# Image-ahead first convolution, one ring for streamed filters and softmax sums by way of HBM in a convolution and attention block

## Chip, core and metric

The kernel runs on one core of a Trainium2 chip. The metric is the device time of one execution in microseconds (us); the times of several runs are compared by their median. Engines are named as the profile names them: PE (matmul), DVE (vector), ACT (activation), POOL and SP (which here issue transfers, POOL also small operations).

## What is computed

Eight images of 512 channels and 32 x 32 pixels, all in float32. Each is group-normalised, sent through a block of convolutions with two attention bottlenecks, and added to its input:

```python
t = cbs(x, cv1_w, cv1_bn, 0)            # 1x1, 512 -> 512; cbs = conv, batch norm, silu
ys = [t[:, :C], t[:, C:]]               # C = 256
for i in range(N):                      # N = 2
    yi = ys[-1]
    z = cbs(yi, m_cv1_w[i], m_cv1_bn[i], 1)          # 3x3, 256 -> 256
    z = bot_attention(z, m_qkv_w[i], m_rw[i], m_rh[i])   # 4 heads of 64, 1024 pixels
    z = jax.nn.silu(bn_eval(conv2d(z, m_cv2_w[i], 0), m_cv2_bn[i]))
    ys.append(yi + z)
y = cbs(jnp.concatenate(ys, axis=1), cv2_w, cv2_bn, 0)   # 1x1, 1024 -> 512
# outside: x = x + y, with y computed from the group-normalised x
```

## The kernel before

Channels lie on the 128 partitions, pixels along the free dimension, in halves of 512 columns. The eight images are unrolled; the order on each engine is made by a scheduler from the code, and the engines run their queues in order. A matmul in float32 is two passes on PE.

Per image the stages are: `gn_stats`, `gn_mean`, `gn_apply` (group norm; L300 to L325: statistics on DVE, two small matmuls gm_ps and gv_ps on PE with `gmat`, a power on POOL, then xn on DVE); `cv1` (L519: 32 matmuls of 512 columns, then silu); two times `bottleneck` (L529); `cv2` (L585: 64 matmuls), which adds x and stores. cv1 makes y0, and y1 in a padded tile `ypad[0]`.

In a bottleneck, `rows_in` (L234) transforms the padded rows on DVE into `v_in`, one tile for each of two input chunks of 128 channels, and the 3x3 convolution is 72 matmuls of 256 columns per output chunk pair (L545) with transformed filters `u`, which are made once (L175 to L193), kept in HBM and streamed through a ring of four slots. `project` (L332) makes q, kr and vT. `attention_fast` (L369) has four groups, one for each head pair and half of the queries, of eight key blocks, taken in pairs: `logits` (PE l_ps, ACT exp into `pt`, DVE adds into `acc`), `times_v` (PE av_ps, then ACT and DVE move it to `ao`), and `divide` (L424 on), which sums `acc` over the keys by matmuls with `ones` (s_ps, L432), adds the halves, keeps their largest and smallest value (smax, smin), takes the reciprocal and multiplies `ao`. Then `m2_ps` (L570) is the 1x1 convolution behind the attention, silu and the addition of the bottleneck's input.

`pt`, `v_in` and xn share a ring of three slots (tag pt). PSUM holds three tiles of two banks (tag big) and one (tag av, for av_ps, c3_end and the group norm). At the end smax and smin decide whether a general path, with the row maximum taken off, is run; with these inputs it is not.

SP issues the loads of x and u, ACT those of the other weights at the start, POOL the stores. The next image's x is loaded and its statistics taken between the output chunks of cv2 (`between`).

Of the kernel before, what the change touches and what calls it, by code (L numbers as in the profile page):

```python
# [49 lines left out]
def kernel(  # L51
# [123 lines left out]
    for n in range(N):  # L175
        for k in range(NM):
            raw = const.tile([P, 9, C], F32, tag="u", name="raw", bufs=4)
            nc.sync.dma_start(raw, m_cv1_w[n, ts(k, P)])
            for oc in range(NM):
                g0, g1, g2 = (raw[:, 3 * r : 3 * r + 3, ts(oc, P)] for r in range(3))  # L180
                u = const.tile([P, NPOS, 3, P], F32, tag="u", name="u_new", bufs=4)
                tmp = act.tile([P, 3, 3, P], F32, tag="pt", name="u_tmp", bufs=3)
                even, odd, wide = tmp[:, 0], tmp[:, 1], tmp[:, 2]
                nc.scalar.mul(u[:, 0], g0, 6.0)
                nc.scalar.mul(u[:, 5], g2, 24.0)
                nc.scalar.mul(odd, g1, -4.0)
                nc.vector.tensor_tensor(even, g0, g2, ALU.add)
                nc.vector.scalar_tensor_tensor(u[:, 1], even, -4.0, odd, ALU.mult, ALU.add)
# [538 lines left out]
```

## Time and profile before

| | |
|---|---|
| Median of 3 runs | 2894.04 us (2889.86 to 2895.5) |
| The profiled execution | 2889.72 us |
| Its span, first to last instruction | 2888.1 us |
| Granted PE clock, mean | 0.971 of full |
| PE busy | 2621.9 us (91%) |
| DVE busy | 1671.8 us (58%) |
| ACT busy | 949.0 us (33%) |
| POOL busy | 73.8 us (3%) |
| Moved by DMA | 130.81 MB |

The span is one profiled execution; its own time is 1.6 us above the span and 4.3 below the median of the runs. Busy times are sums over the span. Ends of matmuls are modelled, so rows of PE overlap by a few tenths; starts and waits are what is read. In a row of the timeline the first number is the start, the second the length, and what stands in brackets is the idle time of that engine before it and what ended it. The number behind a line's mean in the groups is the duration of one instruction in nanoseconds.

### The profile page before, as it was taken

What the parts mean: (1) busy time and instruction counts of PE and PEld (TensorE: products, weight loads), DVE (VectorE), ACT (ScalarE), POOL (GpSimd) and SP (SyncE); (2) the same over time, 40 slices, a digit from 0 to 9 for tenths busy, and PEclk for the clock granted to TensorE, in tenths of its full rate; (3) what the DMA queues carried; (4) which work ended last, traced back from release to release, by engine and by line L of the source; (5) the groups of instructions that cost most, each with busy time, mean ns of one, the idle gap of its engine ahead of it and who ended that gap; (6) DMA issues with size and microseconds to landing.
All of it is one profiled execution on the core that took longest, in us unless ns stands there. A gap on an engine that the chain in (4) does not pass through costs nothing.

```text
span 2888.1 us, 32855 instructions
## 1 busy us (share of the span) xinstructions
PE 2621.9 (91%) x13858; PEld 1319.9 (46%) x13858; DVE 1671.8 (58%) x2244; ACT 949.0 (33%) x1273; POOL 73.8 (3%) x180
## 2 busy tenths in 40 slices
PE   2988999899998999989999899998999989999897
PEld 1636346263463534545355443545345353463633
DVE  5384834847348564575546665466744757438482
ACT  1242422424223332333324242242522515224242
POOL 2000000000000000000000000000000000000000
PEclk9999999999999999999999999999999999999999
DMA  9201011010110101101011000101012010110000
GB/s 357 82 1 66 1 58 66 1 66 1 59 66 1 67 15 44 66 13 54 29 37 59 33 34 30 62 34 62 5 44 79 3 66 1 51 66 1 1 1 31
DMA packets 25084, 130.81 MB, mean 45 GB/s; under 512 B 4449, under 2 KB 4961, under 8 KB 15201
## 3 DMA queue, kind: packets, MB, share of 16 engines
q1 hardware_dynamic: 14400, 97.00, 9.4%
q0 software_dynamic: 6784, 26.25, 2.4%
q10 hardware_dynamic: 3744, 5.37, 0.5%
q8 instruction: 111, 1.82, 0.3%
q14 instruction: 45, 0.36, 0.0%
HBM read 102.40 MB, written 26.21 MB: 45 GB/s over the span
## 4 chain that ended last, share of the span: by engine, by line
issue 57%; PE 26%; DVE 13%; POOL 1%; DMA 1%; ACT 1%; DVEq 0%; POOLq 0%; ACTq 0%; SPq 0%
PE ps L229 12%; PE c_mid L545 6%; DVE acc L401 5%; PE c_end L545 3%; DVE rs L445 3%; PE l_ps L391 2%; PE av_ps L414 2%; PE v_ps L360 2%; DVE acc L398 1%; POOL out_dram L606 1%; DVE rs L441 1%; DVE smin L444 1%; DVE ao L447 1%; ACT pt L395 1%; DVE s L438 1%
## 5 line engine op out<-in xcount | busy, mean ns | idle before, releaser
L395 ACT ACTIVATE pt<-l_ps 128x1024 f32<-128x1024 f32 x512 | 483.0, 1031 | 159.0 <-PE l_ps L391 157.1
L401 DVE TENSOR_TENSOR acc<-acc,pt 128x1024 f32<-128x1024 f32 x384 | 470.2, 1224 | 68.0 <-ACT pt L395 33.7
L414 PE MATMUL av_ps<-pt,vT 64*64 64x512 f32 x4096 | 472.7, 591 | 25.8 <-DVE ao L422 25.8
L391 PE MATMUL l_ps<-q,kr 64*64 64x512 f32 x4096 | 463.3, 590 | 0.0
L545 PE MATMUL c_mid<-v_in,u 128*128 128x256 f32 x1536 | 353.2, 387 | 81.3 <-DVE v_in L265 66.8
L545 PEld LDWEIGHTS c_mid<-v_in,u 128*128 128x128 f32 x1536 | 295.2, 193 | 137.5 <-issue 95.4
L414 PEld LDWEIGHTS av_ps<-pt,vT 64*64 64x64 f32 x4096 | 153.4, 133 | 319.2 <-issue 260.8
L391 PEld LDWEIGHTS l_ps<-q,kr 64*64 64x64 f32 x4096 | 154.5, 132 | 286.7 <-issue 204.3
L229 PE MATMUL ps<-xn,cv_sb 128*128 128x512 f32 x512 | 233.4, 617 | 50.4 <-DVE xn L325 50.4
L214 ACT ACTIVATE h<-ps,bh,sh 128x512 f32<-128x512 f32 x128 | 92.5, 772 | 514.4 <-PE ps L229 514.4
L229 PE MATMUL ps<-z,qkv_sb 128*128 128x512 f32 x512 | 229.2, 595 | 0.2 <-DVE z L558 0.2
L229 PE MATMUL ps<-ypad,cv_sb 128*128 128x512 f32 x512 | 224.9, 592 | 0.0
L445 DVE RECIPROCAL rs<-rs 128x512 f32<-128x512 f32 x64 | 214.6, 3353 | 2.2
L229 PEld LDWEIGHTS ps<-xn,cv_sb 128*128 128x128 f32 x512 | 99.1, 196 | 178.7 <-issue 116.5
L545 PE MATMUL c_end<-v_in,u 128*128 128x256 f32 x768 | 176.1, 382 | 0.0
L545 PEld LDWEIGHTS c_end<-v_in,u 128*128 128x128 f32 x768 | 148.1, 193 | 22.1
L229 PEld LDWEIGHTS ps<-ypad,cv_sb 128*128 128x128 f32 x512 | 97.3, 190 | 122.5 <-issue 122.5
L279 DVE TENSOR_TENSOR sd<-c_mid,m 128x512 f32<-128x512 f32 x32 | 22.1, 692 | 223.3 <-ACT m L277 223.3
L229 PEld LDWEIGHTS ps<-z,qkv_sb 128*128 128x128 f32 x512 | 95.9, 190 | 106.8 <-issue 95.7
L570 PE MATMUL m_ps<-ao,m_sb 128*128 128x512 f32 x256 | 143.7, 714 | 0.9 <-DVE ao L447 0.9
L600 DVE SCALAR_TENSOR_TENSOR t<-t,h 128x512 f32<-128x512 f32 x64 | 41.4, 688 | 164.3 <-ACT t L215 164.3
L351 DVE TENSOR_TENSOR kr<-ps,rw_sb 128x512 f32<-128x512 f32 x64 | 41.2, 686 | 160.4 <-PE ps L229 160.4
(104 smaller groups left out, 2123.7 us busy)
## 6 DMA issues: line engine op xcount, KB each, us to landing
u<-u SPq DMA_DIRECT2D x64, 1152.0 KB, 6.9
x<-in_x_dram SPq DMA_DIRECT2D x32, 512.0 KB, 4.2
out_dram<-t POOLq DMA_DIRECT2D x64, 256.0 KB, 4.3
u<-u_new POOLq DMA_DIRECT2D x8, 1152.0 KB, 7.6
raw<-in_m_cv_w_dram SPq DMA_DIRECT2D x4, 1152.0 KB, 7.8
cv_sb<-in_cv_w_dram ACTq DMA_DIRECT2D x1, 2048.0 KB, 13.5
qkv_sb<-in_m_qkv_w_dram ACTq DMA_DIRECT2D x2, 768.0 KB, 13.1
cv_sb<-in_cv_w_dram ACTq DMA_DIRECT2D x1, 1024.0 KB, 9.4
```

What stands on the lines that cost most here:

```text
L214: nc.scalar.activation(h, ps, AF.Identity, scale=sh[:, k : k + 1], bias=bh[:, k : k + 1])
L229: nc.tensor.matmul(ps[:, half, :], w_of(k), rhs_of(k, half), start=(k == 0), stop=(k == nk - 1))
L351: nc.vector.tensor_tensor(dst, img(ps[:, half, :]), rw, ALU.add)
L360: nc.tensor.matmul(ps[:, j, :], z[:, k, ts(j0 + j, P)], qkv_sb[:, n, k, 2 * C : 3 * C], start=(k == 0), stop=(k == NM - 1),)
L391: nc.tensor.matmul(ps[kh * HD : (kh + 1) * HD, hd, :], kr[r, c, o : o + HD], q[r, c, ts(half, HALF)], start=True, stop=True,)
L395: nc.scalar.activation(pt[:, i], ps, AF.Exp, scale=SCALE)
L401: nc.vector.tensor_tensor(accs[g], accs[g], pt[:, i], ALU.add)
L414: nc.tensor.matmul(avs[g][hd * HD : (hd + 1) * HD, kh, :], vT[r, j, o : o + HD], pt[r, i, hd, :], start=(j == 0), stop=(j == NJ - 1),)
L445: nc.vector.reciprocal(rs, rs)
L545: nc.tensor.matmul(dst, us[k][:, pos, dx, :], vs[k][:, pos, :, dx : dx + F], start=(i == 0), stop=(i == NM * 3 - 1),)
L570: nc.tensor.matmul(pss[oc][:, half, :], m2_sb[:, n, k, ts(oc, P)], ao[:, k, ts(half, HALF)], start=(k == 0), stop=(k == NM - 1),)
L600: nc.vector.scalar_tensor_tensor(t, t, 1.0, h, ALU.add, ALU.mult)
```

## The change

The kernel is rewritten around four things. The normalisation writes into x's own tiles, and `cv1` takes a list of output chunks. Group norm, the load of cv1's filters, and the y1 half of the next image's cv1 are placed in the present image's first attention (`behind`: a table from group number to a function that is called there), the y0 half behind its `m2`; `rows_in` for the next image stands ahead of cv2. There is a third padded tile, since y1 of two images is alive.

cv1's and cv2's filters no longer stay in SBUF: they, `u` and the new `u_new` share one ring of four slots, and are loaded for each image. Filter transforms are made when first needed, from raw pieces in the pt ring. cv2 reads x again for the residual, through POOL's queue.

In `divide`, for all groups but the last of an attention, one row per head of the sums goes to HBM, comes back with 8 sums on each of 128 partitions, is added and inverted there, goes to HBM again and returns broadcast over the 64 partitions of a head. The last group keeps the reciprocal on 128 x 512 and sends its sums only for the final range check. Pairs are taken one ahead (logits of pair i, then the product of pair i - 1) in place of two and two.

```diff
-    xs = [load_x(act, 0, c, 5) for c in range(NX)]
+    xs = [load_x(act, 0, c, NX) for c in range(NX)]
+    def ring(shape, name):
+        return const.tile(shape, F32, tag="u", name=name, bufs=4)
+    def load_w1(q):
+        w = ring([P, NX, 2 * C], "w1")
+        q.dma_start(w, cv1_w.rearrange("(k p) o -> p k o", p=P))
+        return w
+    def load_w2():
+        nk = (2 + N) * NM // 2
+        ws = [ring([P, nk, C2], f"w2_{i}") for i in range(2)]
...
+    def make_u(n, oc, k):
+        raw = act.tile([P, 9, P], F32, tag="pt", name="raw", bufs=3)
+        nc.sync.dma_start(raw, m_cv1_w[n, ts(k, P), :, ts(oc, P)])
...
         def gn_mean(mv):
-            ps = ps_av.tile([P, NX], F32, tag="av", name="gm_ps")
+            ps = ps_big.tile([P, NX], F32, tag="big", name="gm_ps")
...
-            xn = []
-            for half in range(NH):
-                t = act.tile([P, NX, HALF], F32, tag="pt", name="xn", bufs=n_pt)
...
+            for c in range(NX):
+                nc.vector.tensor_scalar(
+                    xts[c], xts[c], gm[:, c : c + 1], gr[:, c : c + 1], ALU.subtract, ALU.mult
+                )
...
-                ps = act.tile([P, HALF], F32, tag="rs", name="s_0", bufs=2)
-                nc.scalar.copy(ps, sums[:, 0])
-                nc.vector.tensor_tensor(ps, sums[:, 1], ps, ALU.add)
                 rs = act.tile([P, HALF], F32, tag="rs", name="rs", bufs=2)
+                dst = ao[:, c, ts(half, HALF)]
                 i = at + g
-                nc.vector.tensor_scalar(
-                    rs, ps, 1.0, None, ALU.mult, ALU.max, accum_out=smax[:, i : i + 1]
-                )
-                nc.vector.tensor_reduce(smin[:, i : i + 1], rs, AX.X, ALU.min)
-                nc.vector.reciprocal(rs, rs)
-                dst = ao[:, c, ts(half, HALF)]
+                s_dram = tc.dram_tile([2, 2, HALF], F32, name=f"s_dram{i}")
+                rows = [act.tile([P, HALF], F32, tag=t, name="s_row", bufs=2) for t in ("h", "t")]
+                for kh, row in enumerate(rows):
+                    nc.scalar.copy(row, ps[:, kh, :])
+                    for hd in range(2):
+                        nc.sync.dma_start(s_dram[kh, hd : hd + 1, :], row[hd * HD : hd * HD + 1, :])
+                if last:
+                    nc.vector.tensor_tensor(rs, ps[:, 1, :], rows[0], ALU.add)
+                    nc.vector.reciprocal(rs, rs)
+                cs = small.tile([P, 2, QP], F32, tag="cs", name="cs", bufs=2)
+                nc.sync.dma_start(cs, s_dram.rearrange("k h (i r) -> (h i) k r", r=QP))
+                nc.vector.tensor_tensor(sums_all[:, i, :], cs[:, 0], cs[:, 1], ALU.add)
+                if not last:
+                    rc = small.tile([P, QP], F32, tag="rc", name="rc", bufs=2)
+                    nc.vector.reciprocal(rc, sums_all[:, i, :])
+                    r_dram = tc.dram_tile([2, HALF], F32, name=f"r_dram{i}")
+                    nc.sync.dma_start(r_dram.rearrange("h (i r) -> (h i) r", r=QP), rc)
+                    for hd in range(2):
+                        nc.sync.dma_start(
+                            rs[hd * HD : (hd + 1) * HD, :], r_dram[hd : hd + 1, :].to_broadcast([HD, HALF])
+                        )
                 nc.vector.tensor_tensor(dst, dst, rs, ALU.mult)
-            RUN = 2
-            for i in range(0, len(pairs), RUN):
...
+            for i in range(len(pairs) + 1):
+                if i < len(pairs):
+                    logits(pairs[i])
+                if i > 0:
+                    times_v(pairs[i - 1])
+                    g, j0 = pairs[i - 1][0]
+                    if j0 == 0:
+                        if g > 0:
+                            divide(g - 1)
+                        behind.get(g, lambda: None)()
+            behind.get(len(groups), lambda: None)()
             divide(len(groups) - 1)
...
+            def residual(oc, half):
+                t = act.tile([P, HALF], F32, tag="xr", name="x_res", bufs=2)
+                nc.gpsimd.dma_start(t, rows_of(x, oc, half))
...
+    s.group_norm(xs)
+    us = {(0, 0): make_u(0, 0, 0), (0, 1): make_u(0, 0, 1), (1, 0): make_u(0, 1, 0)}
+    y0 = new_y0()
+    s.cv1(w1, xs, y0, ypad[0], [*Y1S, *Y0S])
+    vs = [s.rows_in(ypad[0], k) for k in range(NM)]
+    load_bottleneck(0)
     for b in range(B):
...
+        z = s.conv3x3(0, vs, u_of(0))
...
+        if more:
+            xs = [load_x(act, b + 1, c, NX) for c in range(NX)]
+        def ahead():
+            nonlocal w1
+            if more:
+                s.group_norm(xs)
+                w1 = load_w1(nc.sync)
+            for oc, k in ((0, 0), (0, 1), (1, 0)):
+                us[oc, k] = get_u(1, oc, k)
+        def first():
+            nonlocal nxt
+            if more:
+                nxt = new_y0()
+                s.cv1(w1, xs, nxt, y1n, Y1S)
+        ao = s.attention_fast(0, z, b * N * NM * NH, {1: ahead, NM * NH: first})
+        s.m2(0, ao, y1, lambda oc, half: inner(y2, oc, half))
         if more:
+            s.cv1(w1, xs, nxt, y1n, Y0S)
+        vs = [s.rows_in(y2, k) for k in range(NM)]
+        z = s.conv3x3(1, vs, u_of(1))
...
+        ao = s.attention_fast(1, z, (b * N + 1) * NM * NH, {1: ahead})
+        ylast = act.tile([P, NM, HW], F32, tag="v", name="ylast")
+        s.m2(1, ao, y2, lambda oc, half: ylast[:, oc, ts(half, HALF)])
+        if more:
+            vs = [s.rows_in(y1n, k) for k in range(NM)]
+        s.cv2(b, w2, y0, y1, y2, ylast)
```

How the order of the engines' queues moves is shown at three places; line numbers are those of each kernel. First, DVE in the middle of an attention of the kernel before, where one group is divided among the next group's additions:

```order
L398 TENSOR_TENSOR acc<-pt 128x1024
L401 TENSOR_TENSOR acc<-acc,pt 128x1024 x2
L438 TENSOR_TENSOR s_2319<-s_ps,s_2319 128x512
L441 TENSOR_SCALAR rs,smax<-s_2319 128x512
L444 TENSOR_REDUCE smin<-rs 128x1
L445 RECIPROCAL rs<-rs 128x512
L447 TENSOR_TENSOR ao<-ao,rs 128x512
L401 TENSOR_TENSOR acc<-acc,pt 128x1024 x4
```

And DVE of the change at the same place, in a second attention (cs: the sums come back from HBM, rc: their reciprocals, rs: those broadcast):

```order
L429 TENSOR_TENSOR acc<-acc,pt 128x1024 x4
L479 TENSOR_TENSOR sums_all<-cs 128x8
L482 RECIPROCAL rc<-sums_all 128x8
L429 TENSOR_TENSOR acc<-acc,pt 128x1024 x2
L489 TENSOR_TENSOR ao<-ao,rs 128x512
L426 TENSOR_TENSOR acc<-pt 128x1024
L450 TENSOR_TENSOR ao<-av_ps,ao 128x512
```

The division is now in two short pieces, each behind a transfer, and the multiply (L489) stands ahead of the next group's first addition (L426) and of the addition that empties av_ps (L450).

Second, PE at the end of a first attention, of the kernel before (l_ps logits, av_ps product with v, s_ps sums, m_ps the 1x1 convolution behind, c_mid and c_end the 3x3 convolution):

```order
L391 MATMUL l_ps<-q,kr 64x512 x16
L414 MATMUL av_ps<-pt,vT 64x512 x16
L432 MATMUL s_ps<-acc,ones 64x512 x4
L570 MATMUL m_ps<-ao,m_sb 128x512 x8
L545 MATMUL c_mid<-v_in,u 128x256 x3
```

And of the change (ps is the next image's cv1, w its filters):

```order
L419 MATMUL l_ps<-q,kr 64x512 x8
L442 MATMUL av_ps<-pt,vT 64x512 x16
L255 MATMUL ps<-x,w_2473 128x512 x16
L461 MATMUL s_ps<-acc,ones 64x512 x4
L606 MATMUL m_ps<-ao,m_sb 128x512 x6
L255 MATMUL ps<-x,w_2473 128x512 x2
L606 MATMUL m_ps<-ao,m_sb 128x512 x2
L255 MATMUL ps<-x,w_2473 128x512 x14
L584 MATMUL c_mid<-v_in,u 128x256 x24
```

Sixteen matmuls of the next image now stand between the last product and the last sum, and sixteen more around and behind m_ps, ahead of the 3x3 convolution.

Third, DVE of the change at the end of a second attention, from the last pair's additions on (w_tmp and v_in are the next image's rows):

```order
L429 TENSOR_TENSOR acc<-acc,pt 128x1024
L280 SCALAR_TENSOR_TENSOR w_tmp<-ypad_110 128x512
L489 TENSOR_TENSOR ao<-ao,rs 128x512
L283 TENSOR_TENSOR w_tmp<-ypad_110 128x512
L284 TENSOR_TENSOR w_tmp<-ypad_110 128x512
L291 TENSOR_TENSOR v_in<-w_tmp 128x8x32
L292 TENSOR_TENSOR v_in<-w_tmp 128x8x32
L293 SCALAR_TENSOR_TENSOR v_in<-w_tmp 128x8x32
L294 SCALAR_TENSOR_TENSOR v_in<-w_tmp 128x8x32
```

Two more of v_in follow, then the addition that empties av_ps and the last division; in the kernel before these rows stood behind cv1, at the 3x3 convolution.

## Rows read from the trace of the kernel before

**Rows 1.** Page, part 1: busy time, share of the span, instructions of each engine.
```profile
PE 2621.9 (91%) x13858; PEld 1319.9 (46%) x13858; DVE 1671.8 (58%) x2244; ACT 949.0 (33%) x1273; POOL 73.8 (3%) x180
```

**Rows 2.** Timeline of PE, second image: start, length, instruction, idle before it.
```profile
440.65 1.46 PE L545 MATMUL c_mid<-v_in,u 128*128 128x256 f32 x6
...
446.51 9.30 PE L545 MATMUL c_mid<-v_in,u 128*128 128x256 f32 x42 [1.81 <-issue]
...
527.40 1.95 PE L414 MATMUL av_ps<-pt,vT 64*64 64x512 f32 x16 [0.70 <-DVE ao L422]
...
543.09 1.95 PE L414 MATMUL av_ps<-pt,vT 64*64 64x512 f32 x16 [0.86 <-DVE ao L422]
...
547.43 3.61 PE L391 MATMUL l_ps<-q,kr 64*64 64x512 f32 x32
550.86 3.61 PE L414 MATMUL av_ps<-pt,vT 64*64 64x512 f32 x32
558.26 1.09 PE L432 MATMUL s_ps<-acc,ones 64*64 64x512 f32 x8 [3.78 <-DVE acc L401]
...
576.64 2.90 PE L545 MATMUL c_mid<-v_in,u 128*128 128x256 f32 x6 [8.33 <-DVE v_in L265]
...
756.18 3.60 PE L229 MATMUL ps<-ylast,cv_sb 128*128 128x512 f32 x8
759.61 0.28 PE L306 MATMUL gm_ps<-mv,gmat 128*128 128x4 f32 x2
760.74 0.39 PE L317 MATMUL gv_ps<-dev,gmat 128*128 128x4 f32 x2 [0.85 <-DVE dev L312]
763.17 29.57 PE L229 MATMUL ps<-xn,cv_sb 128*128 128x512 f32 x64 [2.05 <-DVE xn L325]
792.58 1.46 PE L545 MATMUL c_mid<-v_in,u 128*128 128x256 f32 x6
```

**Rows 3.** Timeline of PE's weight loads: the sixth m2 matmul of the first attention.
```profile
566.33 0.30 PEld L570 LDWEIGHTS m_ps<-ao,m_sb 128*128 128x128 f32 x2 [0.77 <-DVE ao L447]
```

**Rows 4.** Stretches behind two waits: busy times, then PEclk, DMA share, GB/s.
```profile
558.30:568.40 10.10, 10.01 (x24) 3.63 (x24) 6.53 (x7) 1.46 (x3) 0.00 (x0) 0.83 0.00 0
...
576.70:580.60 3.90, 3.90 (x11) 3.16 (x12) 3.87 (x11) 0.00 (x0) 0.00 (x0) 0.56 0.00 0
```

**Rows 5.** Groups by line and shape: count, busy us, mean ns, idle before.
```profile
L445 DVE RECIPROCAL rs<-rs 128x512 f32<-128x512 f32 x64 | 214.6, 3353 | 2.2
...
L215 ACT ACTIVATE t<-h 128x512 f32<-128x512 f32 x192 | 113.4, 625 | 2.0
...
L214 ACT ACTIVATE h<-ps,bh,sh 128x512 f32<-128x512 f32 x128 | 92.5, 772 | 514.4 <-PE ps L229 514.4
...
L398 DVE TENSOR_TENSOR acc<-pt 128x1024 f32<-128x1024 f32 x64 | 78.1, 1220 | 87.8 <-ACT pt L395 87.8
...
L447 DVE TENSOR_TENSOR ao<-ao,rs 128x512 f32<-128x512 f32 x64 | 44.3, 692 | 2.2
...
L437 ACT COPY s<-s_ps 128x512 f32<-128x512 f32 x64 | 37.5, 585 | 174.9 <-PE s_ps L432 174.9
...
L325 DVE TENSOR_SCALAR xn<-x,gm,gr 128x512 f32<-128x512 f32 x64 | 31.5, 553 | 8.1 <-POOL gr L320 8.1
...
L188 DVE SCALAR_TENSOR_TENSOR u_new<-u_tmp 128x384 f32<-128x384 f32 x8 | 4.4, 555 | 3.0 <-DMA u<-u_new 2.9
```

**Rows 6.** Timeline of the start: the bn power on POOL, cv1's first matmuls on PE.
```profile
19.02 3.10 POOL L162 TENSOR_TENSOR rstd<-rstd,mhalf 128x16 f32<-128x16 f32 x1 [4.53 <-DVE rstd L161]
...
56.99 3.78 PE L229 MATMUL ps<-xn,cv_sb 128*128 128x512 f32 x4 [33.14 <-DVE xn L325]
```

**Rows 7.** Page, part 6: issues of x, KB each, median us to landing.
```profile
x<-in_x_dram SPq DMA_DIRECT2D x32, 512.0 KB, 4.2
```

**Rows 8.** Transfers of u issued in 590:594, one load of 1152 KB.
```profile
DMA to landing us min/median/max: 5.0/5.0/5.0
```

**Rows 9.** Transfers of out in 2825:2889, eight stores of 256 KB.
```profile
DMA to landing us min/median/max: 2.3/3.1/3.7
```

More of the change, by code (lines that the diff above doesn't have):

```diff
@@ L149 @@
     ypad = []
-    for n in range(N):
+    for n in range(N + 1):
         yp = const.tile([P, NM, F + 2, F], F32, name=f"ypad{n}")
@@ L174 @@
     ]
[L175 to L188, printed above, removed]
-                nc.vector.scalar_tensor_tensor(u[:, 2], even, -4.0, odd, ALU.mult, ALU.subtract)
-                nc.vector.scalar_tensor_tensor(wide, g2, 4.0, g0, ALU.mult, ALU.add)
-                nc.vector.scalar_tensor_tensor(u[:, 3], g1, 2.0, wide, ALU.mult, ALU.add)
-                nc.vector.scalar_tensor_tensor(u[:, 4], g1, -2.0, wide, ALU.mult, ALU.add)
-                nc.gpsimd.dma_start(u_dram[n][oc][k], u)
@@ new lines, in make_u @@
+    def make_u(n, oc, k):
+        raw = act.tile([P, 9, P], F32, tag="pt", name="raw", bufs=3)
+        nc.sync.dma_start(raw, m_cv1_w[n, ts(k, P), :, ts(oc, P)])
+        g0, g1, g2 = (raw[:, 3 * r : 3 * r + 3, :] for r in range(3))
+        u = ring([P, NPOS, 3, P], "u_new")
+        tmp = act.tile([P, 3, 3, P], F32, tag="wt", name="u_tmp", bufs=1)
+        even, odd, wide = tmp[:, 0], tmp[:, 1], tmp[:, 2]
+        nc.scalar.mul(u[:, 0], g0, 6.0)
+        nc.scalar.mul(u[:, 5], g2, 24.0)
+        nc.scalar.mul(odd, g1, -4.0)
+        nc.vector.tensor_tensor(even, g0, g2, ALU.add)
+        nc.vector.scalar_tensor_tensor(u[:, 1], even, -4.0, odd, ALU.mult, ALU.add)
+        nc.vector.scalar_tensor_tensor(u[:, 2], even, -4.0, odd, ALU.mult, ALU.subtract)
+        nc.vector.scalar_tensor_tensor(wide, g2, 4.0, g0, ALU.mult, ALU.add)
+        nc.vector.scalar_tensor_tensor(u[:, 3], g1, 2.0, wide, ALU.mult, ALU.add)
+        nc.vector.scalar_tensor_tensor(u[:, 4], g1, -2.0, wide, ALU.mult, ALU.add)
+        nc.gpsimd.dma_start(u_dram[n][oc][k], u)
+        return u
@@ L425, in divide @@
                 c, half = groups[g]
-                sums = ps_big.tile([P, 2, HALF], F32, tag="big", name="s_ps")
+                last = g + 1 == len(groups)
+                ps = ps_big.tile([P, 2, HALF], F32, tag="big", name="s_ps")
                 acc = accs.pop(g)
@@ L577, in bottleneck @@
                     nc.vector.scalar_tensor_tensor(t, t, 1.0, h, ALU.add, ALU.mult)
-                    if n == N - 1:
-                        dst = ylast[:, oc, ts(half, HALF)]
-                    else:
-                        dst = inner(ypad[n + 1], oc, half)
-                    nc.vector.tensor_tensor(dst, t, inner(yi, oc, half), ALU.add)
-            return ylast
-        def cv2(b, y0, ylast, xts, between):
+                    nc.vector.tensor_tensor(dst_of(oc, half), t, inner(yi, oc, half), ALU.add)
@@ L620 @@
+    vs = [s.rows_in(ypad[0], k) for k in range(NM)]
+    load_bottleneck(0)
+    nxt = None
     for b in range(B):
-        y0 = s.cv1(xn)
-        for n in range(N):
-            at = (b * N + n) * NM * NH
-            ylast = s.bottleneck(n, lambda n, z: s.attention_fast(n, z, at))
         more = b + 1 < B
-        if more:
-            nxt = [load_x(act, b + 1, 0, 5)]
-            mv = small.tile([P, NX, 2], F32, tag="mv", name="mv", bufs=2)
-        def between(oc):
-            if not more:
-                return
-            if oc > 0:
-                s.gn_stats(mv, oc - 1, nxt[oc - 1])
-            if oc + 1 < NX:
-                nxt.append(load_x(act, b + 1, oc + 1, 5))
@@ L648 @@
+    nc.vector.tensor_reduce(ends[:, 1:2], flat_sums, AX.X, ALU.min)
     good = const.tile([P, 1], F32, name="good")
```

168 lines of the change are left out of this document (88 added, 80 removed).

## Prediction

> **What bounds the kernel now.** I read the page first, then the PE timeline of the second image, then the clock in its stretches, then the costliest groups by line, and last the start and the DMA landings. The page [rows 1] shows PE busy for 91% and DVE for 58%; a share over stages of unlike limits does not say where PE waits, so the timeline decides. One image lasts from its first 3x3 convolution at 440.65 to the next one's at 792.58, 351.9 us [rows 2]. The reader is to see there that PE waits at five places: 1.81 inside the first 3x3 convolution, 0.70 and 0.86 inside an attention (on the DVE addition that empties av_ps), 3.78 before the last sum (on DVE's acc), 8.33 before the second 3x3 convolution (on v_in), and 0.85 and 2.05 around the group norm. All but the 1.81, whose releaser the row calls issue, end on DVE.
>
> After the long waits the clock falls too: 0.83 of full over the 10.1 us behind the 3.78, 0.56 over the 3.9 us behind the 8.33, so for most of the latter the lower level, 1.2 GHz [rows 4]. Each costs 1.7 us.
>
> DVE is why the attention waits. One division is an add, a reduction with its copy, another reduction, the reciprocal and a multiply: 4 x 0.69 + 3.35 = 6.1 us [rows 5]. With 7 additions of 1.22 and one 0.69 a group (one head pair, 512 queries) takes 15.3 us of DVE, against 8 stretches of 1.72 (half of the 3.43 between the rows at 547.43 and 550.86 [rows 2]) and 0.86 for the sum, 14.6 of PE. The group from 527.40 to 543.09 lasts 15.7.
>
> Before cv1's first matmul lie 56.99 us [rows 6], since all eight filter transforms go ahead of the normalised x on DVE.
>
> **The change, part by part.** Times within an attention count from the end of a group's sum matmuls (s_ps) on PE.
>
> *Start.* DVE now has the normalisation ahead of all but three filter transforms. The bn power ends at 22.1 [rows 6]; the transforms ahead of gm (11 instructions of 0.55 [rows 5], issued once the bn parameters are in, from 19.0 on) end near 25, and from gm to cv1's first matmul 3.6 go by as in the second image (759.61 to 763.17 [rows 2]), 0.5 more for the wider apply: 29.5 in place of 57.0, -27.5. Five transforms move into image 0. Their raw tiles now sit in the ring of the exp tiles (pt), so three of them hold up its first attention: 3 x 6 x 0.55 = 9.9 of DVE and about one more for a raw load that shows, +11.
>
> *Group norm and cv1.* From gm at 759.61 to the convolution at 792.58 are 33.0 us, 64 passes x 0.429 (8 in the 3.43 from 756.18 to 759.61) = 27.5 of it work [rows 2]: -5.5. Instead gm and gv stand in the first attention's PE queue, and gv waits there for DVE as it did (0.85): +1.1.
>
> *The y1 half of cv1 behind the first attention.* Now 11.9 us lie between the last av (550.86 + 3.61) and the sixth m2 matmul, the first that wants the last division (566.33 [rows 3]); 5.15 is work, 6.75 lost. In the new order 16 cv1 matmuls (13.7) come between, but ACT's row copies and DVE's division stand behind the two silus of those outputs: 2 x (0.77 + 0.63) = 2.8 of ACT from cv1's end, then copy 0.59, add 0.69, reciprocal 3.35, multiply 0.69 [rows 5], with hand-overs 8.4. Sum and five m2 matmuls cover 5.15: 3.25 lost, -3.5.
>
> *The y0 half behind m2.* From 566.33 to 576.64 are 10.3, 2.6 of it work; with the slow clock behind it 9.5 are lost. 14 cv1 matmuls (12.0) cover this. But the second chunk's v_in now waits on DVE behind the y0 silus and behind a bn_stats whose x load is released by the same cv1 and takes 4.2 [rows 7]: I take 2.3 left, -7.2. Late next is that chunk. The 1.81 goes, since v_in of the next image is made during the second attention: -1.8.
>
> *One ring for filters.* w1, w2 and u share 4 slots. The late ones (u of the second output chunk, released by cv2's last matmuls) have half a convolution, 72 passes of 0.22 (9.30 for 42 [rows 2]), 15.6 us, against 5.0 to land [rows 8]; cv2's filters are asked for an attention ahead: 0. Without that lead PE would wait the whole landing. Residual x is read again on POOL's queue, a piece of 13.7 us ahead: 0.
>
> *Sums through HBM.* In three of four groups DVE loses 0.69 x 3 + 3.35 = 5.4 us, leaving 9.9 against PE's 14.6: the waits of 0.70 and 0.86 go in both attentions, -3.1 an image. What comes is a chain: ACT copies two rows (0.25 + 2 x 0.59 = 1.4), four transfers each wait for the one before (rows to HBM, cs back, rc to HBM, rs back broadcast), 0.5 of DVE lies in the middle, and 1.1 goes to second issues on SP and the bytes of rs. With h for one hop rs is there at 3.0 + 4h.
>
> DVE's order has the ao multiply that needs rs ahead of the next group's first acc addition and of the ao addition that frees av_ps. Queued behind it are all exps' additions; PE waits for av_ps at 12.0 (seven stretches of 1.72), and DVE needs 0.69 + 1.22 + 0.69 = 2.6 from rs. **So PE's wait is 4h - 6.4** at two places of an attention.
>
> No row has so small a transfer. From below: out (256 KB) lands in 2.3 at best [rows 9], u (1152 KB) in 5.0 [rows 8]; the line through both leaves 1.5 at no bytes. From above: x (512 KB) lands in 4.2 [rows 7], which at that line's 340 GB/s leaves 2.7. I take h = 2.0, nearer the low end, because x shares the DMA with two stores. Then rs is there at 11.0 and the wait is 1.6.
>
> The Trainium skill (DMA: Bandwidth & Descriptors, Specifications) says that pieces below 512 B miss line rate, being done as read-modify-write; cs and rc move 32-byte pieces. If by that rule those two hops took 2.7, the total would be about 2890; no row here shows such a transfer alone.
>
> In the first attention of images 0 to 6 the first division is later: DVE holds the cs addition behind the x apply (3.0 us from gm to its start, the 3.56 above less one of 0.55, and four of some 1.0, twice 0.55 less overlap [rows 5], done at 7.2) and two additions of 1.3, so rc comes at 10.3, rs at 11.0 + 2h = 15.0, and the wait is 15.0 + 2.6 - 13.1 = 4.5, with a clock loss of 1.7 behind it. Behind each 1.6 I allow 0.5, between nothing and 1.7.
>
> At the second attention's end the last division keeps its reciprocal, and DVE makes the next image's v_in between the waits: rs at 11.0 (DVE reaches it at 11.4), multiply, two 0.6, six 0.33, ao addition, division: the sixth m2 matmul 20.6 after s_ps, 12.0 after the last av, as now (11.9): 0.
>
> *Sum.* Per image -1.8 - 5.5 - 3.1 - 3.5 - 7.2 = -21.1 and 3 x 1.6 + 4.5 + 1.1 + 1.7 + 1.5 = +13.6, together -7.5. Seven images -52; the last has no next one to cover it with, 0. Start -27.5 + 11. In all -68.5 from the profiled execution's 2889.7, 2821; the median of the runs lies 4.3 above it: **2825**.
>
> **Rivals.**
> *The hops are hidden* (h = 1.5): no wait at three places (-6.3), one less in the long one, one less at the second attention's end: -15.8 an image, 2766. For it: the 2.3 of out. Against it: SP issues nine transfers a division, POOL two at a time.
> *The hops cost 2.7*, the slower case: each wait is 4.4 (13.2 an image) with a loss of clock like that behind 3.78 (5.1), the long one 7.6, gm 1.1, 2.8 at the second attention's end: 29.8 against 21.1, +8.7 for seven images, some +17 for the last: 2955. It turns slower at h = 2.37. The rule on short pieces points this way.
> *Half of the hops cost 2.7*: the change brings its covers and gives them back, 2890.
> *The cover does not hold*: DVE waits for x in the middle of v_in, and half of the 7.2 stays: 2850. It changes the size, not the sign.
>
> **How the numbers follow.** 0.35 for the forecast, 0.10 for the weaker cover, 0.20 for hidden hops, 0.20 for hops of 2.7, 0.15 for the case between. About 0.2% (6 us) is what a measurement of this kernel can tell from no change. Faster: 0.35 + 0.10 + 0.20 and half of the 0.15, 0.72; same 0.06; slower 0.22. The range takes in hidden hops with room for other waits that shrink, and leaves out half of the slow case: 2740 to 2935. The likeliest case alone spans 2785 to 2865.
>
> **What would show it.** Right: in a middle group the ao multiply starts 10 to 12 us after s_ps; PE waits for the ao addition 1 to 2.5 us at two places an attention and 4 to 5 once; cv1 begins at 28 to 31; no wait over 3 us before the second 3x3 convolution; small landings of 1.8 to 2.2. Wrong: landings of 2.5 or more with PE waits of 4 and a clock below 0.95 within the attention (slower), or below 1.6 with attentions of 58.5 throughout (2766).

## Result and profile after the change

The changed kernel takes 2729.45 us (median of 4 runs, 2725.93 to 2730.7) against 2892.55 before: ratio 0.9434, 95% interval 0.9418 to 0.945. The forecast was 2825 with a range of 2740 to 2935: the sign was right, the gain, 163 us, is more than twice the 68.5 of the sum, and the time lies 10.5 us below the range. The mean granted clock rose from 0.971 to 0.989 of full.

The page, part 1 (busy us, share, instructions), which answers to [rows 1]:

```profile
PE 2595.1 (95%) x13858; PEld 1305.0 (48%) x13858; DVE 1393.7 (51%) x2036; ACT 988.8 (36%) x1337; POOL 106.9 (4%) x248
```

DVE is busy 278 us less: 64 x 1.46 of range reductions (0.69 each and 0.08 to read the first one's result) and 48 x 3.35 of reciprocals make 254 of it. The timeline of PE, start and second image, answers to [rows 2] and [rows 6]:

```profile
29.11 30.08 PE L255 MATMUL ps<-x,w 128*128 128x512 f32 x64 [2.71 <-DVE x L348]
...
402.16 10.52 PE L584 MATMUL c_mid<-v_in,u 128*128 128x256 f32 x48
...
473.10 1.04 PE L461 MATMUL s_ps<-acc,ones 64*64 64x512 f32 x8
474.07 0.39 PE L332 MATMUL gm_ps<-mv,gmat 128*128 128x4 f32 x2
...
490.25 2.76 PE L442 MATMUL av_ps<-pt,vT 64*64 64x512 f32 x16 [2.30 <-DVE ao L450]
...
507.27 1.95 PE L442 MATMUL av_ps<-pt,vT 64*64 64x512 f32 x16 [0.49 <-DVE ao L450]
...
518.59 14.00 PE L255 MATMUL ps<-x,w 128*128 128x512 f32 x32
532.52 1.09 PE L461 MATMUL s_ps<-acc,ones 64*64 64x512 f32 x8
533.53 5.42 PE L606 MATMUL m_ps<-ao,m_sb 128*128 128x512 f32 x12
538.79 1.88 PE L255 MATMUL ps<-x,w 128*128 128x512 f32 x4
541.37 1.98 PE L606 MATMUL m_ps<-ao,m_sb 128*128 128x512 f32 x4 [0.70 <-DVE ao L489]
543.19 12.18 PE L255 MATMUL ps<-x,w 128*128 128x512 f32 x28
...
557.14 9.30 PE L584 MATMUL c_mid<-v_in,u 128*128 128x256 f32 x42 [0.48 <-issue]
...
640.21 1.95 PE L442 MATMUL av_ps<-pt,vT 64*64 64x512 f32 x16 [0.29 <-DVE ao L450]
...
656.70 1.95 PE L442 MATMUL av_ps<-pt,vT 64*64 64x512 f32 x16 [1.67 <-DVE ao L450]
...
669.08 1.09 PE L461 MATMUL s_ps<-acc,ones 64*64 64x512 f32 x8 [0.99 <-DVE acc L429]
...
679.22 3.54 PE L606 MATMUL m_ps<-ao,m_sb 128*128 128x512 f32 x4 [2.84 <-DVE ao L489]
...
736.68 10.52 PE L584 MATMUL c_mid<-v_in,u 128*128 128x256 f32 x48
```

cv1 begins at 29.1 in place of 57.0. The image lasts 334.5 in place of 351.9 (images 2 to 7: 333.4 on average, against 351.7). The wait of 3.78 before the last sum is gone in the first attention and 0.99 in the second; in place of the 8.33 on v_in stands 0.48. The counts in the rows are passes, two for each matmul. The two halves of cv1 stand at 518.59, 538.79 and 543.19 as PE's cover. What is left, beside 0.70 and 0.48, is the four waits for av_ps, 4.75 together, and 0.99 and 2.84 at the second attention's end.

The clock behind the two longer waits (busy times, then PEclk, DMA share, GB/s) answers to [rows 4]:

```profile
490.20:494.40 4.20, 4.15 (x24) 1.33 (x28) 2.36 (x2) 0.00 (x0) 0.00 (x0) 0.63 0.00 0
...
679.20:684.00 4.80, 4.78 (x8) 2.19 (x9) 1.15 (x3) 2.55 (x4) 0.00 (x0) 0.67 0.00 0
```

Each costs some 1.6 us, close to the 1.7 of [rows 4]; behind the waits of 0.29 to 1.67 the matmuls keep full speed.

One trip of sums through HBM, in the first attention's third group (the sums are the second group's; PE's s_ps runs from 492.77 to 494.72), rows of ACT, SP and DVE:

```profile
494.76 1.07 ACT L471 COPY s_row<-s_ps 128x512 f32<-128x512 f32 x2 [5.68 <-PE s_ps L461]
495.38 1.12 SPq L473 DMA_DIRECT2D s_dram<-s_row  x4
...
497.54 0.39 SPq L478 DMA_DIRECT2D cs<-s_dram  x1
...
499.47 0.17 DVE L479 TENSOR_TENSOR sums_all<-cs 128x8 f32<-128x8 f32 x1
499.90 0.34 SPq L484 DMA_DIRECT2D r_dram<-rc  x1
...
501.37 1.09 SPq L486 DMA_DIRECT2D rs<-r_dram  x2
...
504.78 0.69 DVE L489 TENSOR_TENSOR ao<-ao,rs 128x512 f32<-128x512 f32 x1 [2.06 <-DMA rs<-r_dram]
...
505.39 1.22 DVE L426 TENSOR_TENSOR acc<-pt 128x1024 f32<-128x1024 f32 x1
...
506.53 0.68 DVE L450 TENSOR_TENSOR ao<-av_ps,ao 128x512 f32<-128x512 f32 x1
```

This is the picture the prediction drew: rs arrives 10.1 after s_ps, DVE stands 2.06 before L489, and L426 and L450, which frees av_ps, come behind it. With 3.0 + 4h the hop is 1.8 here and 2.05 in the second attention's third group (11.2), so the hop was near the 2.0 taken, and 4h - 6.4 gives 0.7 and 1.8 where 0.49 and 1.67 stand. The mechanism was right. But the wait is a small difference of larger times: 0.2 less a hop halves it.

### The profile page after: what moved, and what is told of

Same layout as the page of the kernel before. It is cut to its first block, busy times and chain, and to the rows that moved or that the text cites. A ratio compares the mean times of both kernels' runs of the same rounds, so it can differ in the third digit from the quotient of the medians.

```text
span 2727.0 us, 33863 instructions
## 1 busy us (share of the span) xinstructions
PE 2595.1 (95%) x13858; PEld 1305.0 (48%) x13858; DVE 1393.7 (51%) x2036; ACT 988.8 (36%) x1337; POOL 106.9 (4%) x248
## 4 chain that ended last, share of the span: by engine, by line
PE 74%; DVE 10%; DMA 9%; ACT 3%; issue 2%; SPq 1%; POOL 0%; DVEq 0%; POOLq 0%; ACTq 0%
PE ps L255 31%; PE c_mid L584 12%; PE av_ps L442 9%; PE l_ps L419 8%; PE c_end L584 6%; DMA rs<-r_dram 4%; PE v_ps L387 4%; DMA r_dram<-rc 2%; DVE acc L429 2%; DVE rs L476 2%; PE s_ps L461 2%; PE m_ps L606 1%; DVE acc L426 1%; DVE ao L489 1%; DMA cs<-s_dram 1%
## 5 line engine op out<-in xcount | busy, mean ns | idle before, releaser
L442 PE MATMUL av_ps<-pt,vT 64*64 64x512 f32 x4096 | 507.8, 597 | 39.4 <-DVE ao L450 39.4
L419 PE MATMUL l_ps<-q,kr 64*64 64x512 f32 x4096 | 502.4, 592 | 4.1 <-ACT pt L423 4.1
L584 PE MATMUL c_mid<-v_in,u 128*128 128x256 f32 x1344 | 298.1, 380 | 10.8 <-DVE v_in L291 8.4
L584 PEld LDWEIGHTS c_mid<-v_in,u 128*128 128x128 f32 x1344 | 254.8, 190 | 55.6 <-issue 20.1
L255 PE MATMUL ps<-x,w 128*128 128x512 f32 x512 | 226.5, 599 | 2.7 <-DVE x L348 2.7
L255 PE MATMUL ps<-ypad,w 128*128 128x512 f32 x512 | 224.9, 592 | 0.0
L255 PEld LDWEIGHTS ps<-x,w 128*128 128x128 f32 x512 | 97.6, 192 | 128.5 <-issue 125.2
L255 PEld LDWEIGHTS ps<-ypad,w 128*128 128x128 f32 x512 | 97.3, 190 | 122.5 <-issue 122.5
L426 DVE TENSOR_TENSOR acc<-pt 128x1024 f32<-128x1024 f32 x64 | 78.2, 1222 | 92.1 <-ACT pt L423 92.1
L593 ACT ACTIVATE t<-z,bh,sh 128x512 f32<-128x512 f32 x64 | 48.6, 806 | 195.5 <-DVE z L321 195.5
```

Of the source, the lines that this page charges most:

```text
L255: nc.tensor.matmul(ps[:, half, :], w_of(k), rhs_of(k, half), start=(k == 0), stop=(k == nk - 1))
L419: nc.tensor.matmul(ps[kh * HD : (kh + 1) * HD, hd, :], kr[r, c, o : o + HD], q[r, c, ts(half, HALF)], start=True, stop=True,)
L426: nc.vector.tensor_tensor(accs[g], pt[:, 0], pt[:, 1], ALU.add)
L442: nc.tensor.matmul(avs[g][hd * HD : (hd + 1) * HD, kh, :], vT[r, j, o : o + HD], pt[r, i, hd, :], start=(j == 0), stop=(j == NJ - 1),)
L584: nc.tensor.matmul(dst, us[k][:, pos, dx, :], vs[k][:, pos, :, dx : dx + F], start=(i == 0), stop=(i == NM * 3 - 1),)
```

## Experiments

Ratios are to the kernel before on the same chip, with 95% intervals. Differences to the kernel before go by the ratio, the others are between medians.

### The division alone, in the kernel before

**e7** puts the changed division alone into the kernel before (two and two, no cover; the range check takes the maximum and minimum of the 128 x 8 sums).

```diff
-                nc.vector.tensor_reduce(smin[:, i : i + 1], rs, AX.X, ALU.min)
-                nc.vector.reciprocal(rs, rs)
...
+                nc.vector.tensor_tensor(tot, cs[:, 0], cs[:, 1], ALU.add)
+                nc.vector.tensor_reduce(smax[:, i : i + 1], tot, AX.X, ALU.max)
+                nc.vector.tensor_reduce(smin[:, i : i + 1], tot, AX.X, ALU.min)
...
+                    nc.vector.reciprocal(rc, tot)
```

> The kernel before with the division of the changed one alone (sums by way of HBM for three of four groups, two and two as it was; the range check reduces the 128 x 8 sums). Theory A': waits of 0.70 and 0.86 at av_ps and 3.78 with 1.7 of clock before the last sum fall to about 0.7 and 0.6, as in the last image of the changed kernel with two and two: 16 x 5.5 = -88, about 2805 us. Theory B' (the trip is worth 7.5 us, the dropped range reductions 1.4 us of DVE a group): 2860 or more.

Measured: 2798.3, ratio 0.9669 (0.9652 to 0.9687), 96 us less. **e9** takes only the range reductions off the division and leaves all reciprocals on DVE; its edit against e7:

```diff
-                last = g + 1 == len(groups)
+                last = True
```

> The kernel before with only the two range reductions (0.69 us each on 128 x 512) and the copy between them taken off the division: the range check uses sums sent through HBM, all reciprocals stay on DVE at 128 x 512. The trip with the reciprocals in it took 95 us off the kernel before. Theory A'' (DVE's 3.35 us reciprocal is what had to go): at most 16 x 1.4 us less at the last sums, about 2870 us. Theory B'' (DVE was over PE's 14.6 us a group by the 1.4 us of the reductions alone; below it, what is saved is worth little): about 2810 us, within 15 of the whole trip's 2798.

Measured: 2843.3, ratio 0.9829 (0.9811 to 0.9847), 50 less. Neither theory holds alone: about half each. PE's waits of the second image, first e7:

```profile
540.29 1.09 PE L434 MATMUL s_ps<-acc,ones 64*64 64x512 f32 x8 [0.69 <-DVE acc L402]
...
547.49 1.98 PE L588 MATMUL m_ps<-ao,m_sb 128*128 128x512 f32 x4 [0.75 <-DVE ao L465]
557.86 2.90 PE L563 MATMUL c_mid<-v_in,u 128*128 128x256 f32 x6 [8.38 <-DVE v_in L266]
```

then e9:

```profile
547.59 1.88 PE L434 MATMUL s_ps<-acc,ones 64*64 64x512 f32 x8 [2.81 <-DVE acc L402]
549.40 8.06 PE L588 MATMUL m_ps<-ao,m_sb 128*128 128x512 f32 x16
565.79 0.76 PE L563 MATMUL c_mid<-v_in,u 128*128 128x256 f32 x1 [8.33 <-DVE v_in L266]
```

In both the 0.70 and 0.86 of [rows 2] are gone. In e9 the last sum still waits 2.81 and s_ps and m2 behind it run slow (clock 0.84 of full over 10.5 us); in e7 the wait is 0.69, and s_ps and m2 behind it are at full speed (1.00 over 8.8). That takes 0.70 + 0.86 + 3.09 = 4.65 of waits from an attention, 74 us in all (a new 0.75 at m2 in the first attentions takes 6 back); the rest of the 96, some 1.7 an attention, is put down to the clock. In e7's second image no wait for rs shows, as with two and two av_ps is asked for later; over all eight images seven are left, 4.8 us together.

### One pair ahead, with and without the trip

**e1** is the changed kernel with all four reciprocals on DVE at 128 x 512 (the same one line as e9); **e2** the changed kernel with pairs two and two; **e5** has both edits.

```diff
-            for i in range(len(pairs) + 1):
-                if i < len(pairs):
-                    logits(pairs[i])
-                if i > 0:
-                    times_v(pairs[i - 1])
+            RUN = 2
+            for i in range(0, len(pairs), RUN):
+                for pair in pairs[i : i + RUN]:
+                    logits(pair)
+                for pair in pairs[i : i + RUN]:
+                    times_v(pair)
```

> The changed kernel with the reciprocal of all four groups on DVE (add, 3.35 us reciprocal and multiply on 128 x 512); the sums still go through HBM, but only for the range check. Theory A (the DVE time that the trip through HBM saves is what made the attentions shorter than forecast): the waits of before come back, 0.7 and 0.9 for av_ps and 3.8 before the last sum with 1.7 of lost clock, 7 us an attention, against about 2.5 of waits for rs that go: 16 x 4.5 = +72, about 2800 us. Theory B (the order with one pair ahead made them shorter, and the trip only costs its hops): the waits for rs go and nothing comes back, 16 x 2.5 less, about 2690. In between: both have a part.

> The changed kernel with pairs taken two and two again (logits of two pairs, then the products of both), all else as changed. Theory A (DVE time saved): DVE has 10 us of work in a group of 14.6, so the order matters little: 2729 within 15. Theory B (order): the additions of two pairs stand together again before the last sum, its wait of 3.8 and the clock behind it come back, 5.5 us an attention at least: 16 x 5.5 = +88, about 2815.

> The changed kernel with both: reciprocals of all groups on DVE, and pairs taken two and two. With the runs so far it completes a square (trip through HBM or not, one or two pairs). Theory A' (the trip is worth much, but only where two pairs stand together and its hops are hidden): DVE has 14.1 us in a group of 14.6 and is late before the last sum again by 2.4 to 3.8 with 1.7 of clock, and a little at av_ps; against the trip with two and two (2697) that is 16 x 4 = +64, about 2760 us. Theory B' (the trip is worth next to nothing in either order, as with one pair ahead, where it is 7.5 us; what helped is that the two range reductions left DVE): 2697 to 2710.

| changed kernel | trip through HBM | all on DVE |
|---|---|---|
| one pair ahead | 2729.45 (0.9434) | e1 2737.0 (0.9459; 0.9443 to 0.9475) |
| two and two | e2 2696.5 (0.9317; 0.93 to 0.9335) | e5 2706.1 (0.9348; 0.9331 to 0.9365) |

e1 lies between its theories: once the range reductions are off DVE and the other parts are in, the trip is worth 7.5 us in one order and 9.6 in the other, where e7 less e9 has 45. With one pair ahead it brings waits for rs in place of those it removes. e1, second attention of the second image:

```profile
639.12 1.95 PE L442 MATMUL av_ps<-pt,vT 64*64 64x512 f32 x16 [0.49 <-DVE ao L450]
654.44 1.95 PE L442 MATMUL av_ps<-pt,vT 64*64 64x512 f32 x16 [0.49 <-DVE ao L450]
669.81 1.19 PE L461 MATMUL s_ps<-acc,ones 64*64 64x512 f32 x8 [3.98 <-DVE acc L429]
```

e2 went against both of its theories: two and two is 33 us faster than one pair ahead. e5 lies in its theory B'. Why the trip is worth so little here shows at the second attention's end, first e5:

```profile
661.92 1.98 PE L461 MATMUL s_ps<-acc,ones 64*64 64x512 f32 x8 [3.62 <-DVE acc L429]
```

then e2:

```profile
659.82 1.09 PE L461 MATMUL s_ps<-acc,ones 64*64 64x512 f32 x8 [1.50 <-DVE acc L429]
...
670.43 2.83 PE L607 MATMUL m_ps<-ao,m_sb 128*128 128x512 f32 x4 [2.99 <-DVE ao L489]
```

What the trip takes off the last sum comes back at m2: from the last product with v to the next image both need 69.6 us on average over images 2 to 7. At the first attention's end, under cv1, both have 36.7. So the two places where e7 gained most are taken: one by the cover, the other by something that stands ahead of the last division (see below). **e6** is the order alone, in the kernel before (the same edit backwards).

> The kernel before with one pair ahead in place of two and two, nothing else. If one pair ahead costs by itself (in the changed kernel it costs 33 us, 2 an attention): 2894 + 16 x 2 = about 2925 us. If it only costs where the trip through HBM is, and helps where the additions of two pairs pile up before the last sum (3.8 and 1.7 of clock, 5.5 an attention): about 2830.

Measured: 2909.6, ratio 1.0053 (1.0035 to 1.0071), 15 slower, half of what the first theory had: av_ps waits 1.46 twice an attention for 0.70 and 0.86, s_ps 3.25 for 3.78. The order costs in both kernels.

### The wait for rs in DVE's order

**e4** lengthens the chain by a copy from HBM to HBM.

```diff
+                    r2_dram = tc.dram_tile([2, HALF], F32, name=f"r2_dram{i}")
+                    nc.sync.dma_start(r2_dram, r_dram)
+                    r_dram = r2_dram
```

> The changed kernel with one more hop in the chain: the reciprocals are copied from HBM to HBM before they are broadcast. DVE's order is unchanged. If the chain of hops sets the waits for av_ps (theory of the prediction, wait = 4h - 6.4 with h now read as 1.8): each of four waits an image grows by the whole hop, and the third multiply in the second attention by part of it: 4 to 5 x 1.8 plus lost clock of up to 1.7 at each, 8 to 15 us an image, 2795 to 2850 us. If DVE's own queue sets them (the hop is hidden behind additions): under 2745.

Measured: 2828.3, ratio 0.978 (0.9759 to 0.98): 99 us more, within what the chain of hops gave: 11.6 an image on average in images 2 to 7, and 24 in the last, which has no cover. SP's rows of one trip, and PE's waits of the second image:

```profile
508.89 0.50 SPq L486 DMA_DIRECT2D r_dram<-r_dram  x1
510.80 1.10 SPq L489 DMA_DIRECT2D rs<-r_dram  x2
```

```profile
497.96 3.31 PE L442 MATMUL av_ps<-pt,vT 64*64 64x512 f32 x16 [4.32 <-DVE ao L450]
516.83 1.95 PE L442 MATMUL av_ps<-pt,vT 64*64 64x512 f32 x16 [2.34 <-DVE ao L450]
...
652.88 3.69 PE L442 MATMUL av_ps<-pt,vT 64*64 64x512 f32 x16 [3.40 <-DVE ao L450]
673.56 1.95 PE L442 MATMUL av_ps<-pt,vT 64*64 64x512 f32 x16 [2.92 <-DVE ao L450]
```

The hop takes 1.9, and the four waits grow by 2.02, 1.85, 3.11 and 1.25, 2.06 on average (2.04 over all eight images): the hop lies in PE's path whole. **e8** leaves the chain and moves the wait: the multiplies of the first two groups are issued on DVE behind the addition that frees av_ps.

```diff
-                    nc.vector.tensor_tensor(dst, av[:, 1], dst, ALU.add)
+                    moved = nc.vector.tensor_tensor(dst, av[:, 1], dst, ALU.add)
+                    if g - 1 in scales:
+                        with tc.issue_after(moved.ins):
+                            scales.pop(g - 1)()
```

> The changed kernel with the multiply by rs of the first two groups issued on DVE behind the addition that frees av_ps, in place of ahead of it. If DVE waiting in order for rs is what PE's waits for av_ps come from: they fall to the 0.49 that stands also without any trip (one 1.22 addition ahead of the one that frees av_ps), 4.75 and about 1 of clock an image become 2: 8 x 3.7 = -30, about 2700 us. If the waits come from the additions in DVE's queue: 2729 within 8.

Measured: 2679.0, ratio 0.9255 (0.9239 to 0.9272), 50 less. The gain is more than the 30 expected: no wait for av_ps of 0.25 or more is left in any image, so the 0.49 was no floor. PE's waits left in the second image are:

```profile
532.11 1.98 PE L613 MATMUL m_ps<-ao,m_sb 128*128 128x512 f32 x4 [0.70 <-DVE ao L492]
547.89 9.30 PE L591 MATMUL c_mid<-v_in,u 128*128 128x256 f32 x42 [0.48 <-issue]
657.46 1.09 PE L464 MATMUL s_ps<-acc,ones 64*64 64x512 f32 x8 [1.04 <-DVE acc L429]
668.10 3.09 PE L613 MATMUL m_ps<-ao,m_sb 128*128 128x512 f32 x4 [2.99 <-DVE ao L492]
```

### Cover and group norm

**e3** puts both halves of the next image's cv1 behind cv2 again, v_in after them; **e12** moves the group norm there too, ahead of cv1 (its line below is in e12 alone). In both the load of cv1's filters moves to the second attention, and one tile of u fewer is asked for ahead.

```diff
-                s.cv1(w1, xs, nxt, y1n, Y1S)
...
-            s.cv1(w1, xs, nxt, y1n, Y0S)
...
+            s.group_norm(xs)
+            s.cv1(w1, xs, nxt, y1n, [*Y1S, *Y0S])
+            vs = [s.rows_in(y1n, k) for k in range(NM)]
```

> The changed kernel with both halves of the next image's first convolution behind cv2 again; its group norm and apply stay in the first attention. The last image of the changed kernel has no cover and shows the price: waits of 1.07 and 0.76 at m2 and 8.38 on v_in with about 2 of clock behind, against 0.70 and 0.48 in a covered image, 11 us; and about 1.5 for v_in behind the convolution at the image's start. 7 x 12.5 = +87: about 2816 us. Rival (DVE's spare time, not the cover, made the places cheap): under 2770.

> The kernel without cover (2776) with the group norm behind cv2 too: gm, gv and the apply stand between cv2 and the first convolution as in the kernel before. If placing the group norm in the attention is a gain of its own, as the prediction had it (5.5 of waits and lost clock an image against 1.1 for gm and gv in the attention): 7 x 4.4 = +31, about 2807 us. If the apply in the attention costs about as much as it saves (gm and gv 1.5, the first wait for av_ps 2.3 in place of some 0.4, lost clock behind it 1.7): 2776 to 2785.

Measured: e3 2775.9, ratio 0.9591 (0.9571 to 0.961); e12 2789.4, ratio 0.9639 (0.9621 to 0.9658). e3 lies between its theories, e12 just above its second. The cover is worth 47 us, 6.6 an image, not 12.5 (of which 1.5 for the image's start did not come: e3 has no such wait); the group norm's place 13. PE in e3's second image, the two ends of attention:

```profile
542.67 2.90 PE L584 MATMUL c_mid<-v_in,u 128*128 128x256 f32 x6 [8.38 <-DVE v_in L291]
...
658.65 4.56 PE L606 MATMUL m_ps<-ao,m_sb 128*128 128x512 f32 x10 [0.24 <-DVE ao L489]
```

The first end pays 8.38 and the slow clock as expected. The second is better than in the changed kernel: 0.24 for 0.99 and 2.84. So the cover takes away some 10 us an image at the first attention and costs 4 to 5 at the second (10.5 and 4.5 by the starts of rows, images 2 to 7). DVE's rows of the changed kernel there show why:

```profile
668.86 0.68 DVE L280 SCALAR_TENSOR_TENSOR w_tmp<-ypad 128x512 f32<-128x512 f32 x1
669.94 0.69 DVE L489 TENSOR_TENSOR ao<-ao,rs 128x512 f32<-128x512 f32 x1 [0.40 <-DMA rs<-r_dram]
...
673.43 0.42 DVE L296 SCALAR_TENSOR_TENSOR v_in<-w_tmp 128x256 f32<-128x256 f32 x1
673.77 0.69 DVE L450 TENSOR_TENSOR ao<-av_ps,ao 128x512 f32<-128x512 f32 x1
...
675.09 3.35 DVE L476 RECIPROCAL rs<-rs 128x512 f32<-128x512 f32 x1
```

v_in for the next image, not wanted for 60 us, stands ahead of the last division; L450 had its av_ps copied by ACT at 668.75 and runs 5 us later.

### Versions faster than both

**e10** is e8 with the next image's v_in issued behind that division; **e11** the same with two and two. Beside the edit of e8 both have:

```diff
+            with tc.issue_after(done.ins):
                 vs = [s.rows_in(y1n, k) for k in range(NM)]
```

> The changed kernel with the late multiply of the run before it (2679) and the next image's v_in on DVE issued behind the second attention's last multiply, in place of ahead of the last division. If v_in standing in DVE's queue is what PE waits for at the end of the second attention: waits of 1.04 before the last sum and 2.99 at m2 with about 1.7 of clock fall to at most 0.7, 7 x 5 = -35, about 2645 us. If the last division's own length (copy, add, reciprocal, multiply, 6 us) sets the wait: within 10 of 2679.

> The same with pairs taken two and two. Two and two was 33 us faster than one ahead while DVE waited in order for rs. If that wait was the whole of the difference: within 8 of the same kernel with one pair ahead, about 2645. If two and two is better in itself: 2630 or less; if the additions of two pairs before the last sum (0.6 to 1.5) cost: 2655 to 2665.

Measured: e10 2649.0, ratio 0.916 (0.9144 to 0.9177); e11 2648.5, ratio 0.9154 (0.9136 to 0.9172). v_in's place is worth 30 us, and with multiply and v_in late the two orders are the same. It is the multiply that does it: e8's attentions, 59.3 and 57.6 us on average, are already as long as e11's, where the changed kernel has 64.5 and 59.5 and e2 60.2 and 58.1. So DVE's wait for rs was the whole of the 33 us between the orders. An image takes 322.4 (e10) and 322.6 (e11); the clock is 0.994 to 0.996. Both are 3% below the changed kernel.

## Why the prediction was wrong

The terms of the sum can be set against both traces, stage by stage. The stages are read from rows (the first c_mid of a convolution, the first l_ps of an attention, the end of its last av_ps), on average over images 2 to 7; cv1's work (27.5) is taken out where it stands.

| stage | before | after | measured | forecast |
|---|---|---|---|---|
| first 3x3 convolution and projections | 54.1 | 52.0 | -2.1 | -1.8 |
| first attention, to its last product with v | 59.6 | 64.5 | +4.9 | +7.8 |
| from there to the second convolution | 22.4 | 9.3 | -13.1 | -10.7 |
| second convolution and projections | 53.7 | 52.7 | -1.1 | in the line above |
| second attention, to its last product with v | 59.6 | 59.5 | -0.2 | +2.6 |
| from there to the next image | 74.8 | 68.1 | -6.7 | -5.5 |
| one image | 324.2 | 306.0 | -18.2 | -7.5 |

The image lengths are the 351.7 and 333.4 from above less cv1. The forecasts for the attentions hold the waits of before that go (-1.6 each), the new ones (2.1 for each of three, 6.2 for the first) and 1.1 for gm and gv. Seven such images make 75 of the 93 us by which the profiled execution lies under the sum; the last image makes 13, the start most of the rest.

**The step that failed is the size of the waits for rs.** The sum put them at 3 x 1.6 + 1.5 and 4.5 + 1.7, 12.5 an image, 87 in all. e8, which takes them away, gains 50, 7 an image. The place and the law were right, the numbers were not. The law is a difference, 4h - 6.4, and with h at the 1.8 of most trips in place of 2.0 it gives 0.8: the three waits of an image with a next one are 0.78 on average over the seven (0.25 to 1.67). No clock is lost behind those of the second image, where 0.5 was allowed at each. The first wait, put at 4.5, is 2.30 there, as rc comes 8.7 after s_ps where 10.3 was taken (the four applies are done at 6.0, not 7.2); the 1.6 of clock behind it came as forecast. DVE's relief inside the attentions was allowed for: without the waits for rs (e8) the second attention takes 57.6 where the kernel before has 59.6.

**What is left uncovered behind the first attention** was put at 3.25 and 2.3 and is 0.70 and 0.48. The hand-over of 8.4 held: cv1 ends at 532.5, the m2 matmul that wants the last division starts 8.8 later. But the row of [rows 3] belongs to the seventh m2 matmul, not the sixth (twelve passes of m2 stand ahead of it), and in the order shown ahead of the prediction two cv1 matmuls stand before it as well. So sum, six m2 and two cv1 matmuls cover 7.7, not 5.15. Of the 2.3, which was for DVE waiting on an x load, nothing came: DVE's bn_stats there starts without a wait, at 554.2. The relief from the reciprocals is not needed for this: e1, with all of them on DVE, has 0.70 and 0.48 too.

**The division's relief** was credited only where av_ps waits, "the waits of 0.70 and 0.86 go in both attentions, -3.1 an image"; the 3.78 before the last sum stayed where it was. By itself that is far too little: that wait is DVE's lateness, gathered over the groups, that comes due at the last sum. e9 shows a quarter of the 3.78 going with the reductions, e7 nearly all with the reciprocals, and with them the slow clock, 6.0 us an attention against the forecast's 1.56. In the changed kernel the omission costs less, since 14 of the 16 last sums have something else there: in the first attentions cv1 hides the wait anyway, and at the end of the second ones v_in comes between, as the prediction saw ("20.6 after s_ps"). Its 0 there is close: 1.2 an image better. The last image has neither cover nor v_in; forecast at 0, it is 13.4 shorter (324.2 from its first 3x3 convolution to the end of the span, 337.6 before), with both waits of 3.78 gone. What v_in holds back, e10 shows: issued behind the division, it gives 30 us.

**The cover and the group norm** held at their places: e3 to the changed kernel gives 10.5 where 10.7 was forecast, e12 to e3 6.1 where 5.5 was. The price elsewhere is what the sum booked under other terms: 4.5 at the second attention's end (v_in), and 4.9 in the first attention for gm, gv and the applies (1.1 and the excess of the first wait for rs, 4.1). The 1.81 goes, but not for the reason given: it is gone in e12 and e3 too, where v_in is made behind cv1 as before, but y1 ahead of y0.

**Start and filters** held in part: cv1 begins at 29.1 against 29.5; the first image is longer than the next six by 9.7, but in the kernel before it was so by 2.3, so 7.4 stand against 11.

**The order of pairs** had no term of its own, only the place where av_ps is asked for. By itself it costs 15 us (e6).

The runs also make a ladder from one kernel to the other. What a step is worth depends on those above it; the start is read from traces (e12 begins its first 3x3 convolution 29.0 earlier than e7, and its first image is 10.8 longer against its next six than e7's).

| step | us |
|---|---|
| division (e7; of it the reductions -50, e9) | -96 |
| start, filters on demand | -18 |
| rest of e12 less e7: waits for rs, order of pairs, order of cv1's outputs, shared ring | +9 |
| group norm in the attention (e12 to e3) | -13 |
| cover by cv1 (e3 to changed) | -47 |

The steps add up to -165; measured against each other the two kernels are 163 apart.

Of the rivals, hidden hops (2766) came nearest in time, but for another cause: the hops are not hidden, e4's 1.9 came back whole. SP issues eight transfers a trip (4, 1, 1 and 2 in the rows above), not nine. Hops of 2.7 throughout did not happen. The rule of the Trainium skill (DMA: Bandwidth & Descriptors, Specifications) that pieces below 512 B miss line rate pointed that way; by the trace, cs (32-byte pieces) is used 1.93 after its issue and the next transfer issues 1.47 after that of rc, where rows of 2 KB take 1.7 from the end of the last copy to the issue of cs. No run sends these bytes in longer pieces, so what the rule costs here is open. Also open is which part of e12 less e7 belongs to the shared ring: it was not tried alone. Nor was the cover tried with the old division.

## What to carry to other kernels

A forecast wait that is a small difference of larger times needs a range, not a value: 0.2 us in a hop of 2.0 halved it here. A wait at the end of a stage that ends on a busy engine can be lateness gathered over the stage: set that engine's work per round against the bound of the round, and credit relief to the wait where it comes due, its clock loss included, in every repetition where nothing else takes that place. An operand that comes by a long way should be awaited on an in-order engine behind whatever frees a buffer for another engine: moving two multiplies an attention was worth 50 us, where the trip that they wait for had brought 7.5. Work that is given as cover brings followers: here the scheduler put v_in into DVE's gaps ahead of the last division, which cost 30 us; look at what such work stands ahead of.

## What the runs showed that was not expected

Two orders that differ by 33 us (e2 against the changed kernel) are equal to 0.5 us once the multiplies and v_in are moved (e10, e11). A chain of four dependent transfers takes 8.6 to 10.5 us from the last row copy to rs in the trips without an apply between, mostly about 8.9. A hop is 1.4 to 2.5 us in most trips, with 3.7 as the longest (rs at 654.2, second image; the kernel's first trip apart), whether the pieces are rows of 2 KB, of 32 bytes or a copy within HBM (1.9). The Trainium skill (DMA: Bandwidth & Descriptors, Anatomy of one DMA — SWDGE (gpsimd) path) gives a transfer on GpSimd's queue a fixed part of some 2.0 us, with the time of the bytes on top; these hops are on SP's queue, for which the section gives no such figure, and lie near it. And waits of 0.3 to 1.7 us left PE's granted clock at full in the second image, while those of 2.3 and 2.84 were followed by stretches at 0.63 and 0.67.
